# A decoder layer on one core: a quarter of the dense expert placed between the first two experts, the last additions on VectorE, the last outputs loaded into other buffers

## The chip, the core and the metric

The kernel runs on one core of a Trainium2 chip. A core has five engines with queues of their own: TensorE (PE; its weight loads are PEld), VectorE (DVE), ScalarE (ACT), GpSimd (POOL) and SyncE (SP), which here only starts DMAs. The metric is the device time of one execution in microseconds; the median of several executions is given.

## What is computed

One pre-norm decoder layer over 16 x 64 = 1024 tokens of width 256: self-attention with block-scaled weights, cross-attention over a context with rotary embedding, and a mixture-of-experts feed-forward part. Only the last part matters here:

```python
scores = softmax(xt @ Wg.T)                 # 16 experts
topi = top_k(masked by the best 2 of 4 groups, 4)
h = silu(einsum('td,eid->eti', xt, W1)) * einsum('td,eid->eti', xt, W3)
y = einsum('etd,te->td', einsum('eti,edi->etd', h, W2), combine)
z = silu(xt @ Ws1.T) * (xt @ Ws3.T) @ Ws2.T
return y + z                                # added to x
```

Each token is served by 4 of the 16 experts. `y` is the sum of their outputs with the routing weights.

## The kernel before

The tokens lie in eight tiles of 128 rows, `x[0]` to `x[7]`, two halves of four. All products are made of float32 numbers split into a high part (rounded) and a low part (the rest): a product of two is three matmuls, so each matrix that TensorE reads has to be cast by ScalarE (`parts_of`, `weight_parts`) and subtracted by VectorE or GpSimd.

Fifteen of the sixteen experts work on gathered rows. GpSimd scatters each token's normalized row to slots of the expert (`xd` in DRAM, `send`, line 842), 384 slots for each; expert `e` loads its slots (`expert_inputs`, line 1253), turns them on TensorE (line 1265), multiplies them with its up-weights (`expert_hidden`, line 1273), multiplies with its down-weights (`expert_output`), and scatters the result rows to `yd` in DRAM (`send_outputs`, line 1291). `yd` holds, for each token, its four choices. They are loaded back (`load_outputs`, line 1314) and added to `x` with their routing weights (`add_outputs`, line 1327).

The sixteenth expert, `w_last`, is the dense expert: it is computed for all tokens and added with a weight that is zero where it was not chosen (`add_last`, line 952). Its first half is done before the expert loop. The second half is two quarters of 256 tokens, `dense_hidden(w_last, 1, 0)` and `dense_hidden(w_last, 1, 1)`. Quarter 0 adds to `x[4]` and `x[5]`, quarter 1 to `x[6]` and `x[7]`.

The loop `for e in range(E + 1)` (line 1353) is a software pipeline: at step `e` it prepares the inputs and weights of expert `e`, does the up-products of expert `e-1`, and the outputs of expert `e-2`. The instructions are placed by a scheduler that models the engines; `tc.issue_after(ins)` keeps what stands in its block behind an instruction in that order. `up_done[0]` is the last up-product made so far, `gated[0]` the last instruction of `expert_hidden`, `lows[-1]` the last subtraction of a low part.

Three kinds of buffers matter:

- accumulators for up-products, `mm`, four banks, of which an expert takes three;
- accumulators for outputs, `av`, two banks (`av_tile`), which are used by `send_outputs` and by `dense_output`;
- `got`, nine buffers of 256 rows each, for the outputs that are loaded back (16 loads in all, so the last seven wait for a buffer); `w123`, two buffers of 128 x 1280 for raw expert weights, each free once the weights have been cast and subtracted.

Up to nine loads can run ahead. The loads of choice `k` depend on all scatters of `yd` so far (`behind(got, returned)`); the last choice's loads depend on the last expert's scatter. All of them are started from SP's queue.

Of the kernel before, what the change touches and what calls it, by code (L numbers as in the profile page):

```python
# [25 lines left out]
F32 = mybir.dt.float32  # L26
# [3 lines left out]
AF = mybir.ActivationFunctionType  # L30
ALU = mybir.AluOpType
AX = mybir.AxisListType

B, S, D = 16, 64, 256
NT = B * S
NI = NT // 128
# [6 lines left out]
E, INTER, NGRP, TOPK, TOPKG = 16, 176, 4, 4, 2  # L43
# [4 lines left out]
W_COLS = W_UP + 2 * D  # L48
# [23 lines left out]
def decoder_layer(ctx: ExitStack, tc: tile.TileContext, a: dict, out: bass.AP):  # L72
    nc = tc.nc
# [17 lines left out]
    def av_tile():  # L91
        return ps_av.tile([128, 512], F32, tag="av", name="av")
# [18 lines left out]
    def parts_of(src, hi, lo, eng=None):  # L111
        nc.scalar.copy(hi, src)  # L112
        return (eng or nc.vector).tensor_tensor(lo, src, hi, ALU.subtract).ins
# [3 lines left out]
    x = [t[:, i, :] for t in x_pairs for i in range(2)]  # L117
# [131 lines left out]
    def behind(read, writes):  # L249
        for w in writes:  # L250
            tc.add_manual_dep(
                read,
                w.name,
                mybir.DependencyInfo(mybir.DependencyClass.Sync, mybir.DependencyReason.DATA),
                reason="it reads rows of each",
            )
# [29 lines left out]
    def expert_up(w, xs, n):  # L286


        ps = [mm_tile(cols=n) for _ in range(3)]
        return ps, [expert_up_part(k, w, xs, t) for k, t in enumerate(ps)][-1]  # L290
# [8 lines left out]
    def expert_output(ps, w, h_p, cols):  # L299


        w2 = [[p[:, W_UP + k * D : W_UP + (k + 1) * D] for p in w] for k in range(2)]
        h = [p[:, cols] for p in h_p]
        return matmuls(
            ps,
            [
                (h[0], w2[0][0]),
                (h[0], w2[0][1]),
                (h[1], w2[0][0]),
                (h[2], w2[1][0]),  # L310
                (h[2], w2[1][1]),
            ],
        )

    with ExitStack() as attn:
# [643 lines left out]
        with (  # L959
# [109 lines left out]
            def dense_weights():  # L1069

                parts = [
                    xw.tile([128, 2, 2, 4 * HQ], F32R, tag=f"w_q{n}", name=f"w_last{n}")
                    .rearrange("p a b c -> p (a b c)")[:, :W_COLS]
                    for n in range(2)
                ]
                up = xb.tile([128, 3, 2, 2, DC], F32, tag="w_s", name="w_last_up")
                down = xb.tile([128, 2, D], F32, tag="w_o0", name="w_last_down")
                for t, cols in (
                    (up.rearrange("p a b c d -> p (a b c d)"), slice(0, W_UP)),
                    (down.rearrange("p a b -> p (a b)"), slice(W_UP, W_COLS)),  # L1080
                ):
                    nc.sync.dma_start(out=t, in_=a["W123"][E - 1][:, cols])
                    parts_of(t, parts[0][:, cols], parts[1][:, cols])
                return parts
# [18 lines left out]
            def dense_gated(g, up, g2, up2):  # L1103
                h_p = [
                    xa.tile([128, 512], F32R, tag=f"roped1{n}", name=f"dense1{n}", bufs=1)
                    for n in range(2)
                ]
                h_p.append(xa.tile([128, 512], F32R, tag="q_r", name="dense2"))
                nc.vector.tensor_tensor(g, up, g, ALU.mult)
                parts_of(g, h_p[0], h_p[1])  # L1110
                nc.vector.tensor_tensor(g2[:64], up2[64:], g2[64:], ALU.mult)
                parts_of(g2[:64], h_p[2][:64], h_p[2][64:])
                return h_p
# [15 lines left out]
            for n in range(len(units) + 2):  # L1129
# [58 lines left out]
                if n == 8:  # L1188
                    w_last = dense_weights()
                    with after(exps[-1]):  # L1190
                        routed.append(weights_of_choices(0))
                if n == 9:
# [30 lines left out]
                    with after(aimed, placed):  # L1223
# [4 lines left out]
                        h_p = dense_gated(*dense_ups)  # L1228
# [4 lines left out]
    fw = ctx.enter_context(tc.tile_pool(name="fw", bufs=2, reuse_waits="tile"))  # L1233
    fx = ctx.enter_context(tc.tile_pool(name="fx", bufs=2, reuse_waits="tile"))
    fh = ctx.enter_context(tc.tile_pool(name="fh", bufs=2, reuse_waits="tile"))
    fy = ctx.enter_context(tc.tile_pool(name="fy", bufs=2, reuse_waits="tile"))

    gated, up_done = [None], [None]
# [34 lines left out]
    def expert_hidden(w, xs, n):  # L1273


        ps, up_done[0] = expert_up(w, xs, n)
        g, h, g2, h2 = (
            fh.tile([128, SLOTS], F32, tag=tag, name=tag)[:, :n] for tag in ("g", "h", "g2", "h2")
        )
        h_p = [  # L1280
            fh.tile([128, SLOTS], F32R, tag=tag, name=tag)[:, :n] for tag in ("hp0", "hp1", "hp2")
        ]
        nc.scalar.activation(g, ps[0], AF.Silu)
        nc.vector.tensor_tensor(h, ps[1], g, ALU.mult)
        parts_of(h, h_p[0], h_p[1])
        silus.append(nc.scalar.activation(g2[64:], ps[2][:64], AF.Silu).ins)
        nc.vector.tensor_tensor(h2[:64], ps[2][64:], g2[64:], ALU.mult)
        gated[0] = parts_of(h2[:64], h_p[2][:64], h_p[2][64:])
        return h_p
# [23 lines left out]

    def load_outputs(k):

        tiles = []
        for n in range(NI // 2):
            t = fy.tile([128, 2, D], F32, tag="got", name="got", bufs=9)
            first = (E - 1) * SLOTS + (TOPK - 1 - k) * NT + n * 256
            got = nc.sync.dma_start(  # L1320
                out=t, in_=yd[first : first + 256].rearrange("(i p) d -> p i d", p=128)
            ).ins
            behind(got, returned)
            tiles.append(t)
        return tiles

    def add_outputs(k, got, cw):
        for i in range(NI):
            y, w = got[i // 2][:, i % 2], cw[i // 4][:, k, i % 4 : i % 4 + 1]
            if i % 3 == 2:  # L1330
                nc.scalar.activation(y, y, AF.Copy, scale=w)
                nc.gpsimd.tensor_tensor(x[i], x[i], y, ALU.add)
            else:
                nc.vector.scalar_tensor_tensor(x[i], y, w, x[i], ALU.mult, ALU.add)  # L1334

    def dense_hidden(w, half, n):
        return expert_hidden(w, [p[:, :, n * 256 : n * 256 + 256] for p in normed[half]], 256)

    def dense_output(w, h_p, half, n, add):
        for b in range(2):  # L1340
            ps = av_tile()[:, :D]
            expert_output(ps, w, h_p, slice(b * 128, b * 128 + 128))
            add(half, 2 * n + b, ps)
# [6 lines left out]
    ws, xs, hs, got = {}, {}, {}, {}  # L1350
    with tc.issue_after(lows[-1]), tc.issue_after(silus[-1]):
        ws[0] = expert_weights(a["W123"][0], nc.vector)
    for e in range(E + 1):
        if e in (1, 2):

            low = lows[-1]
            hs[e - 1] = expert_hidden(ws[e - 1], xs[e - 1][0], SLOTS)
        if e < E - 1:
            low = lows[-1]
            with tc.issue_after(up_done[0] if e in (1, 2) else low):  # L1360
                xs[e] = expert_inputs(e)
            if e >= 1:
                with tc.issue_after(low), tc.issue_after(silus[-1]):
                    ws[e] = expert_weights(a["W123"][e], nc.vector if e < 3 else nc.gpsimd)
        if e == 1:
            with tc.issue_after(gated[0]), tc.issue_after(silus[-1]):
                routed.append(weights_of_choices(1))
        if 0 <= e - 1 < E - 1 and e > 2:
            hs[e - 1] = expert_hidden(ws[e - 1], xs[e - 1][0], SLOTS)
        if e - 2 >= 0:  # L1370
            if e == E:

                with tc.issue_after(gated[0]):
                    h_p = dense_hidden(w_last, 1, 0)
            last = send_outputs(e - 2, ws.pop(e - 2), hs.pop(e - 2), xs.pop(e - 2)[1])
            if e - 2 == E - TOPK - 2:
                short = slots_are_short()
            k = e - 2 - (E - 1 - TOPK)
            if k >= 0:
                got[k] = load_outputs(k)  # L1380
    with ExitStack() as behind_last:
        for ins in (*last, gated[0]):
            behind_last.enter_context(tc.issue_after(ins))
        cw = [r[0] for r in routed]
        add_outputs(0, got[0], cw)
        dense_output(w_last, h_p, 1, 0, add_last)
        add_outputs(1, got[1], cw)
        dense_output(w_last, dense_hidden(w_last, 1, 1), 1, 1, add_last)
        for k in range(2, TOPK):
            add_outputs(k, got[k], cw)  # L1390
    for i in range(NI):
        (nc.sync if i % 2 == 0 else nc.scalar).dma_start(
# [10 lines left out]
    with tc.If(short > 0):  # L1403
        w_over = [weights_without_slot(half, routed[half][2]) for half in range(2)]
        with tc.For_i(0, E - 1, 1) as e:
            w = expert_weights(a["W123"][bass.ds(e, 1)].rearrange("o p c -> p (o c)"))
            for half in range(2):
                dense_expert(w, half, add_over)

                t = fs.tile([128, 4, E], F32, tag="slot", name="w_next")  # L1410
# [105 lines left out]
```

## Time and profile before

| What | Value |
|---|---|
| median of 3 runs | 580.62 us (577.94 to 586.16) |
| profiled execution, its own time | 577.4 us |
| span of the profiled execution | 575.5 us |
| mean granted TensorE clock | 0.978 |
| first expert's up-products begin | 454.54 us |
| second expert's up-products begin | 463.24 us |
| third expert's up-products begin | 471.41 us |
| first addition of a loaded output | 552.59 us |
| last scatter of expert outputs started | 556.00 us |
| VectorE's last addition ends | about 571.2 us |

Times inside the profile count from the start of the span. In the profile's lines L104 is the helper through which nearly all matmuls go, so that one has to look at the tiles: `mm<-xs,w` are an expert's up-products, `mm<-xn,w_last` those of the dense expert, `av<-w,hp` an expert's outputs, `av<-w_last,hp` the dense expert's. A number in brackets at the end of a line is the time for which the engine was idle before it, and what ended that.

### The profile page before, as it was taken

To read this page: it belongs to the slowest core of one execution; us is meant where nothing else is said; L and a number is where in the kernel's file an instruction comes from. 1 tells how busy PE (TensorE), PEld (TensorE's weight loads), DVE (VectorE), ACT (ScalarE), POOL (GpSimd) and SP (SyncE) were. 2 spreads that over 40 slices of the span, in tenths; PEclk is the share of its full clock that TensorE was granted. 3 is DMA by queue.
4 is the path that set the end of the run, shared out by engine and by line. 5 is a ranking of instruction groups with operands and counts; after the bars stand their busy time and mean duration, and the time that the engine had idled before them with its cause. 6 is when DMAs were issued, how large, how long until landed. Compare 5 with 4: busy or idle time off the path is not lost.

```text
span 575.5 us, 10603 instructions
## 1 busy us (share of the span) xinstructions
PE 540.3 (94%) x4013; PEld 446.7 (78%) x4013; DVE 400.2 (70%) x879; ACT 279.3 (49%) x524; POOL 230.6 (40%) x213
## 2 busy tenths in 40 slices
PE   7999999999999989999999999999999779999962
PEld 5889898888989876757778577685787669999951
DVE  6355566644655788848577586889777479999866
ACT  4677557575574431230432323152525187777551
POOL 4260500101001005426243444632544717888862
PEclk9999999999999999999999999999999789999995
DMA  8564431823200599482020000000511658777384
GB/s 227 145 166 146 111 109 39 227 86 112 75 1 1 167 250 308 111 239 52 2 70 1 8 1 1 0 31 0 188 50 68 202 169 285 240 245 238 122 279 152
DMA packets 56294, 70.83 MB, mean 123 GB/s; under 512 B 13872, under 2 KB 42768, under 8 KB 56240
## 3 DMA queue, kind: packets, MB, share of 16 engines
q1 hardware_dynamic: 51408, 58.71, 34.5%
q0 software_dynamic: 3696, 10.36, 4.7%
q10 hardware_dynamic: 1136, 1.05, 0.6%
q8 instruction: 33, 0.54, 0.4%
q14 instruction: 21, 0.17, 0.1%
HBM read 48.61 MB, written 21.86 MB: 122 GB/s over the span
## 4 chain that ended last, share of the span: by engine, by line
PE 81%; DVE 7%; issue 4%; DMA 3%; ACT 3%; POOL 1%; SPq 1%; DVEq 0%; ACTq 0%; POOLq 0%
PE mm L104 47%; PE mm L1005 7%; PE av L590 5%; PE av L104 5%; PE at L573 4%; PE at L343 3%; PE at L1028 2%; PE av L1041 2%; PE at L1265 2%; PE mm L439 2%; DMA bqkv<-in_bqkv 1%; PE mm L461 1%; DMA got<-yd 1%; DVE x L1334 1%; POOL roped L990 1%
## 5 line engine op out<-in xcount | busy, mean ns | idle before, releaser
L990 POOL TENSOR_TENSOR roped<-rt,rt 128x512 f32<-128x512 f32 x48 | 62.6, 1325 | 83.4 <-DVE rt L984 80.5
L984 DVE TENSOR_TENSOR rt<-mm,rope_q 128x512 f32<-128x512 f32 x96 | 61.4, 685 | 24.3 <-PE mm L104 23.6
L104 PE MATMUL mm<-xn,w_q 128*128 128x512 f32 x288 | 73.9, 403 | 0.5 <-ACT xn L222 0.5
L104 PEld LDWEIGHTS mm<-xn,w_q 128*128 128x128 f32 x288 | 52.2, 188 | 14.0 <-issue 1.8
L104 PE MATMUL mm<-xs,w 128*128 128x384 f32 x270 | 55.3, 354 | 7.0 <-ACT xs L112 5.8
L1304 POOL DMA_INDIRECT yd<-y,to x45 | 47.9, 1064 | 27.6 <-ACT y L1299 13.1
L104 PEld LDWEIGHTS mm<-xs,w 128*128 128x128 f32 x270 | 48.4, 198 | 9.0 <-ACT xs L112 6.6
L327 ACT ACTIVATE p<-p 128x512 f32<-128x512 f32 x32 | 20.1, 629 | 62.3 <-DVE p L326 62.3
L324 DVE TENSOR_REDUCE sm_m<-at 128x8 f32<-128x512 f32 x32 | 21.8, 680 | 37.1 <-PE at L573 36.2
L1005 PE MATMUL mm<-roped,w_s 128*64 128x512 f32 x192 | 46.4, 602 | 0.7 <-POOL roped L990 0.7
L522 POOL TENSOR_TENSOR wv<-code,scale 128x512 fp32r<-128x512 f32 x7 | 9.5, 1360 | 88.2 <-DMA scale<-in_scales 58.7
L613 DVE TENSOR_TENSOR x<-mm,x 128x256 f32<-128x256 f32 x64 | 26.0, 419 | 23.9 <-PE mm L104 21.9
L104 PE MATMUL mm<-wo,o 128*128 128x256 f32 x256 | 39.6, 295 | 0.0
L104 PE MATMUL av<-w,hp 128*128 128x256 f32 x225 | 35.2, 290 | 0.7 <-ACT y L1299 0.7
L104 PE MATMUL mm<-xn,wq 128*128 128x512 f32 x128 | 34.6, 405 | 0.7 <-ACT xn L222 0.5
L104 PE MATMUL mm<-wv,xn 128*128 128x256 f32 x256 | 35.2, 289 | 0.0
L104 PE MATMUL mm<-xn,wk 128*128 128x512 f32 x128 | 34.9, 404 | 0.0
L590 PE MATMUL av<-pt,v 128*128 128x128 f32 x256 | 34.5, 277 | 0.0
L104 PEld LDWEIGHTS mm<-wo,o 128*128 128x128 f32 x256 | 32.9, 190 | 1.5 <-issue 0.4
L590 PEld LDWEIGHTS av<-pt,v 128*128 128x128 f32 x256 | 32.0, 191 | 1.2
L104 PEld LDWEIGHTS mm<-wv,xn 128*128 128x128 f32 x256 | 31.8, 189 | 0.9
L104 PEld LDWEIGHTS av<-w,hp 128*128 128x128 f32 x225 | 30.6, 190 | 1.9 <-ACT y L1299 1.2
(216 smaller groups left out, 1145.8 us busy)
## 6 DMA issues: line engine op xcount, KB each, us to landing
w<-in_W SPq DMA_DIRECT2D x15, 640.0 KB
code<-in_codes SPq DMA_DIRECT2D x32, 256.0 KB
scale<-in_scales SPq DMA_DIRECT2D x32, 256.0 KB
xr<-xd SPq DMA_DIRECT2D x15, 408.0 KB
xd<-zeros SPq DMA_DIRECT2D x8, 720.0 KB
yd<-zeros SPq DMA_DIRECT2D x8, 512.0 KB
got<-yd SPq DMA_DIRECT2D x16, 256.0 KB
wq<-in_Wq SPq DMA_DIRECT2D x4, 512.0 KB
```

The source lines that it names most:

```text
L104: m = nc.tensor.matmul(ps, lhsT=l, rhs=r, start=(n == 0), stop=(n == len(pairs) - 1))
L324: nc.vector.tensor_reduce(m, sc, AX.X, ALU.max)
L327: exps.append(nc.scalar.activation(p, p, AF.Exp, scale=scale).ins)
L343: last = nc.tensor.transpose(ps[:, 2 * n : 2 * n + 2, :].rearrange("p a q -> p (a q)"), pn[:, 2 * n : 2 * n + 2, :].rearrange("p a k -> p ...
L439: nc.tensor.matmul(ps[:, c * DCQ : (c + 1) * DCQ], lhsT=wq[:, h, c * 128 : (c + 1) * 128], rhs=wkq[:, h, :], start=True, stop=True,)
L573: nc.tensor.matmul(sc[par * 64 : par * 64 + 64, 2 * g + pp, :], lhsT=qk[0][:, b * S : (b + 1) * S], rhs=qk[1][:, b * S : (b + 1) * S], sta ...
L590: nc.tensor.matmul(av[:, k * 128 : (k + 1) * 128], lhsT=v[:, i, k0 : k0 + HD], rhs=pt[:, i].rearrange("p a q -> p (a q)"), start=True, sto ...
L613: nc.vector.tensor_tensor(x[i], ps, x[i], ALU.add)
L984: nc.vector.tensor_tensor(mt, ps3, rope_table(t, 2 * ab + k), ALU.mult)
L990: nc.gpsimd.tensor_tensor(r.rearrange("p (b s) -> p b s", s=S), one, two, op)
L1005: nc.tensor.matmul(ps[h // 2][(h % 2) * 64 : (h % 2) * 64 + 64], lhsT=w_s[:, t, blk, ab, :], rhs=roped[2 * t + ab], start=first[h], stop=l ...
L1304: sent = nc.gpsimd.indirect_dma_start(out=yd[: (E - 1) * SLOTS + min(TOPK, E - 1 - e) * NT], out_offset=bass.IndirectOffsetOnAxis(ap=to[:, ...
```

## The change

One quarter of the dense expert (tokens of `x[4]` and `x[5]`) moves: its up-products now stand behind the first expert's, its outputs ahead of the first expert's outputs. The other quarter takes the place that the first one had beside the last expert. All additions of loaded outputs are done by VectorE; before, every third one was a scaling on ScalarE and an addition on GpSimd. The last choice's outputs are loaded into the two raw weights' buffers, four loads of which two start from ScalarE's queue. The order of the additions at the end is changed accordingly. The number of loads, additions and products stays the same.

```diff
     def load_outputs(k):
 
-        tiles = []
-        for n in range(NI // 2):
-            t = fy.tile([128, 2, D], F32, tag="got", name="got", bufs=9)
+        if k == TOPK - 1:
+            tiles = [
+                t[:, n * 2 * D : (n + 1) * 2 * D].rearrange("p (i d) -> p i d", i=2)
+                for t in (fw.tile([128, W_COLS], F32, tag="w123", name="got_last") for _ in range(2))
+                for n in range(2)
+            ]
+        else:
+            tiles = [
+                fy.tile([128, 2, D], F32, tag="got", name="got", bufs=9) for _ in range(NI // 2)
+            ]
+        for n, t in enumerate(tiles):
             first = (E - 1) * SLOTS + (TOPK - 1 - k) * NT + n * 256
-            got = nc.sync.dma_start(
+            got = (nc.scalar if k == TOPK - 1 and n % 2 else nc.sync).dma_start(
                 out=t, in_=yd[first : first + 256].rearrange("(i p) d -> p i d", p=128)
             ).ins
             behind(got, returned)
-            tiles.append(t)
         return tiles
 
     def add_outputs(k, got, cw):
         for i in range(NI):
             y, w = got[i // 2][:, i % 2], cw[i // 4][:, k, i % 4 : i % 4 + 1]
-            if i % 3 == 2:
-                nc.scalar.activation(y, y, AF.Copy, scale=w)
-                nc.gpsimd.tensor_tensor(x[i], x[i], y, ALU.add)
-            else:
-                nc.vector.scalar_tensor_tensor(x[i], y, w, x[i], ALU.mult, ALU.add)
+            nc.vector.scalar_tensor_tensor(x[i], y, w, x[i], ALU.mult, ALU.add)
...
             hs[e - 1] = expert_hidden(ws[e - 1], xs[e - 1][0], SLOTS)
+            if e == 1:
+                with tc.issue_after(up_done[0]):
+                    h_p = dense_hidden(w_last, 1, 0)
...
             if e == E:
 
                 with tc.issue_after(gated[0]):
-                    h_p = dense_hidden(w_last, 1, 0)
+                    h_p = dense_hidden(w_last, 1, 1)
+            if e == 2:
+                dense_output(w_last, h_p, 1, 0, add_last)
             last = send_outputs(e - 2, ws.pop(e - 2), hs.pop(e - 2), xs.pop(e - 2)[1])
...
         cw = [r[0] for r in routed]
-        add_outputs(0, got[0], cw)
-        dense_output(w_last, h_p, 1, 0, add_last)
-        add_outputs(1, got[1], cw)
-        dense_output(w_last, dense_hidden(w_last, 1, 1), 1, 1, add_last)
-        for k in range(2, TOPK):
+        dense_output(w_last, h_p, 1, 1, add_last)
+        for k in range(TOPK):
             add_outputs(k, got[k], cw)
```

## The prediction

> **What bounds the kernel now.** I read the page's busy rows first, then busy time by stage, then the engines' timelines at the two places that the change touches, then the waits.
>
> ```profile
> PE 540.3 (94%) x4013; PEld 446.7 (78%) x4013; DVE 400.2 (70%) x879; ACT 279.3 (49%) x524; POOL 230.6 (40%) x213
> ```
>
> TensorE is the bound over the span as a whole, but two stages differ from that mean. Busy time by stage (stage, its length, then busy time and count of PE, PEld, DVE, ACT, POOL; granted clock; DMA share; GB/s):
>
> ```profile
> 459.20:463.20 4.00, 0.81 (x7) 0.57 (x5) 1.95 (x3) 2.28 (x5) 1.69 (x2) 1.00 0.62 210
> 463.20:469.20 6.00, 5.88 (x26) 5.65 (x27) 4.35 (x17) 4.49 (x7) 0.00 (x0) 0.72 0.71 249
> ...
> 484.00:540.00 56.00, 55.22 (x377) 54.07 (x377) 52.91 (x90) 41.49 (x88) 46.76 (x38) 1.00 0.68 229
> ...
> 560.00:566.00 6.00, 1.99 (x6) 1.43 (x6) 5.87 (x10) 2.08 (x5) 3.10 (x4) 0.50 0.75 232
> 566.00:571.20 5.20, 1.22 (x4) 0.93 (x4) 5.12 (x12) 0.51 (x1) 0.95 (x1) 0.50 0.48 159
> ```
>
> From 484 to 540 us TensorE has no slack: what arrives late there stays late. Between the first two experts it stands idle for 3.2 us. After 560 us VectorE (5.87 of 6.00, 5.12 of 5.20) sets the end. The idle stretch in TensorE's timeline, and ScalarE's work in it:
>
> ```profile
> 459.19 0.82 PE L1265 MATMUL at<-ident,xr 128*128 128x128 f32 x6
> 463.24 0.79 PE L104 MATMUL mm<-xs,w 128*128 128x384 f32 x3 [3.23 <-ACT xs L112]
> ...
> 471.41 0.80 PE L104 MATMUL mm<-xs,w 128*128 128x384 f32 x3 [1.10 <-ACT xs L112]
> ```
> ```profile
> 460.57 0.48 ACT L1286 ACTIVATE g<-mm 64x384 f32<-64x384 f32 x1 [1.33 <-PE at L1265]
> 461.08 1.26 ACT L278 CAST w<-w 128x1280 fp32r<-128x1280 f32 x1
> 462.70 0.48 ACT L112 CAST xs<-at 128x384 fp32r<-128x384 f32 x1 [0.37 <-remote]
> ```
>
> The second expert's up-products wait for its cast rows, which stand in ScalarE's queue behind the first expert's second silu and a weight cast. In the tail, VectorE beside GpSimd, and the loads of the last choice:
>
> ```profile
> 552.59 3.65 DVE L1334 SCALAR_TENSOR_TENSOR x<-got,cw,x 128x256 f32<-128x256 f32 x9
> ...
> 563.39 1.83 DVE L1334 SCALAR_TENSOR_TENSOR x<-got,cw,x 128x256 f32<-128x256 f32 x2
> ```
> ```profile
> 563.22 1.71 POOL L1332 TENSOR_TENSOR x<-x,got 128x256 f32<-128x256 f32 x2 [0.88 <-DVE x L952]
> ```
> ```profile
> 561.03 1.90 SPq L1320 DMA_DIRECT2D got<-yd  x4
> ```
> ```profile
> 564.62 0.51 ACT L1331 ACTIVATE got<-got,cw 128x256 f32<-128x256 f32 x1 [2.43 <-DMA got<-yd]
> 566.12 0.51 ACT L1331 ACTIVATE got<-got,cw 128x256 f32<-128x256 f32 x1 [1.00 <-DMA got<-yd]
> ```
>
> An addition alone takes 0.41 us (3.65 for nine), beside a GpSimd addition 0.92 (1.83 for two). The last choice's loads start at 561.03, once the last expert's scattered rows have landed; the second of them lands at 564.6, the third at 566.1, and the fourth, by the same step, near 566.8. VectorE ends at 571.2, the stores at 575.5.
>
> **Part 1, the quarter moved forward.** It issues 18 up-products and 10 output products of 256 columns, two silus, two casts and six VectorE instructions. At the end 18 such products took 2.32 us, about 0.12 each, so 28 are 3.3 us of TensorE. In the built order the 18 follow the first expert's up-products and precede the second's transposes: 459.3 to 461.4, then transposes until 462.1. The idle time is not filled to its end, because ScalarE's queue grows too: after the silu that ends at 461.05 come the expert's first cast (0.5), the quarter's first silu (0.36), the expert's second cast (0.5) and the quarter's second silu (0.38). The last of these waits for TensorE; the silu at 460.57 came 1.2 us after its products, so I let this one start at 462.6. Then weight cast (1.26), the quarter's cast (0.41), rows cast (0.48): 465.1 instead of 463.18. The second expert's products begin 1.9 us late. Its low half waits for VectorE, where the weights' subtractions (1.56) now end near 465.8.
>
> A second wait is new. The quarter's two outputs take both of the output accumulators, and release them through two VectorE additions (0.4 each) that stand behind the second expert's silus and the last routing weights. The first expert's 15 output products, of which 10 ran in gaps between 463.9 and 472.4, all come after that, near 472. That is 1.2 us of TensorE (10 at 0.12) pushed past the same gaps.
>
> Bounds for the delay with which TensorE reaches the full loop: 0 if all 3.3 us fit in the 3.23 and 1.10 of idle time; +3.3 if none does. I take +2.0, near the 1.9 of the ScalarE sum. From the third expert's products on, the order on every engine is as before, so the delay is carried through to 552. SP's queue keeps its order; the fourth expert's weight load (464.36) waits for a raw buffer that comes free 1.9 us later, and is not used until the cast at 473.25, nine us after it: nothing. If that cover were gone, it would cost those 1.9 us again.
>
> The clock: TensorE was granted 0.72 in 463.20:469.20, right behind the 3.23 us of idleness, which costs 6.0 x 0.28 = 1.7 us. [...] By the row, a gap remains (462.1 to about 464.7), a further one stands near 471, and even a 3.23 us gap brought the drop: sum +2.0. I use the row and keep -1.7 for the range.
>
> **Part 2, additions by VectorE alone.** Removed: 8 of 32 additions on GpSimd with their ScalarE scalings, 2 of 4 dense additions of the tail, four gating instructions (0.42 each) on VectorE. Added: 8 additions on VectorE. Its tail is now 34 x 0.405 = 13.8 us. Before, it was busy 5.43 + 5.87 + 5.12 = 16.4 of the 18.6 us from 552.6 to 571.2. From 552.6 work alone would end at 566.4, a gain of 4.8. ScalarE and GpSimd lose work on which only the scaled additions and the stores of their rows waited.
>
> Waits decide instead. Six additions run until 555.0; the second dense output needs an accumulator freed by the copy at 555.35, so VectorE passes its addition near 557.5. The second choice's last loads landed at 557.85 and 558.6 before; the third choice's four are in by about 562, as two of them no longer wait for buffers that GpSimd had to release (issued about 1.5 us earlier). So all but the last choice is added by about 563.3, the last pair of the third choice apart.
>
> **Part 3, the last loads.** The raw weights' buffers are free since GpSimd's last subtraction (542.81 + 1.34), so these loads wait only for the scattered rows, at 561.0 as before. ScalarE has nothing behind them but stores. [...] four issues in 1.90 us are halved, at most 0.95 gained[...]. The row has 232 GB/s in this stage, 1 MB, so the last landing is bandwidth more than issue. Without any gain the fourth lands at 566.8, and four additions end the work at 568.4 (-2.8); with the full 0.95 at 567.5 (-3.7). The third choice being out of the way earlier also frees bandwidth, so I take -3.7; bounds -1 (landings 1.7 us later, as four loads meet) and -4.8 (VectorE's work alone). The last stores take 4.3 us either way.
>
> **Sum.** 575.5 + 2.0 - 3.7 = 573.8 us of span, -0.3%. The profiled execution took 577.4 us including 1.9 around its span, 3.2 below the median of 580.62. In proportion: 580.62 x 573.8 / 575.5 = 579.
>
> **Rivals.** (a) *The gap swallows the quarter and the clock stays up*: delay 0, clock -1.7, tail -4.8: -6.5, median 574. For it: 4.3 us of idle time against 3.3 of work. Against: ScalarE's queue is what TensorE waits for, and it gets longer. (b) *Slower: the first output accumulators become the wait.* TensorE stands behind two VectorE additions near 470 to 472, which stand behind two table loads (1.28 each) and two silus. No work is absorbed (+3.3) and a further 6.8 us at half speed costs 3.4; the tail, held by landings, gives -2.7: +4.0, median 585. It decides once the loop is entered more than 3.7 us late. Against it: the same 1.1 us gap at 470.3 brought no drop of clock. (c) *The tail does not do what it says*: all four last loads share the same bandwidth, land late, and VectorE waits: -1 and +2.0, median 581.6.
>
> **Numbers.** Forecast 0.60 (own range 575.5 to 582.5), (a) 0.13, (b) 0.17, (c) 0.10. The three times shown lie 1.4% apart, which adds about 2 us either way, so the range is 573.5 to 585.5. About 2% (11.6 us) is what a measurement of this kernel tells from no change. No case reaches it; I leave 0.05 on either side for what the trace doesn't show, such as the clock at half speed in the full loop.
>
> **What would show it.** Right: TensorE idle near 462 to 464.7 with the quarter's products ahead of it; the second expert's products at about 465; the loop about 2 us late at 484; no VectorE addition of 0.8 us or more in the tail; the last addition 3 to 4 us closer to the last expert's scatter. Wrong: the second expert's products before 464 or after 467; VectorE idle for over 3 us after the scatter has landed; the last loads landing over 6 us after their issue.

## The result, and the profile after

| | before | after |
|---|---|---|
| median of 20 executions each | 577.22 us | 581.04 us |
| span of the profiled execution | 575.5 us | 579.2 us |
| first expert's rows turned on TensorE (begin) | 451.61 us | 453.27 us |
| second expert's up-products begin | 463.24 us | 467.11 us |
| fifth expert's up-products, the group of 13, begin | 484.06 us | 489.44 us |
| last scatter's issue ends | 557.07 us | 562.37 us |
| last choice's loads begin to be issued | 561.03 us | 567.71 us |
| VectorE's last addition ends | about 571.2 us | 574.74 us |

The ratio is 1.0073 (95% interval 1.0059 to 1.0087): the change costs 4.2 us, where the forecast had a gain of 1.7. The medians in this table are of all executions, and the ratio leaves out those that ran in a slower state, some 10 us longer (5 of 20 before, 3 of 20 after). TensorE is the bound over the span as before, in the first row of busy times of the page:

```profile
PE 539.9 (93%) x4013; PEld 447.6 (77%) x4013; DVE 400.2 (69%) x887; ACT 275.6 (48%) x516; POOL 224.6 (39%) x205
```

The same stages as in the prediction, the last one drawn out to VectorE's new end (stage, its length, busy time and count of PE, PEld, DVE, ACT, POOL; granted clock; DMA share; GB/s):

```profile
459.20:463.20 4.00, 4.00 (x19) 4.00 (x18) 0.97 (x2) 1.40 (x4) 1.92 (x2) 0.61 0.53 168
463.20:469.20 6.00, 4.15 (x28) 3.39 (x27) 5.07 (x11) 5.05 (x10) 0.00 (x0) 1.00 0.41 130
484.00:540.00 56.00, 55.19 (x383) 54.34 (x382) 52.17 (x88) 41.54 (x87) 45.27 (x38) 1.00 0.73 242
560.00:566.00 6.00, 0.69 (x5) 0.48 (x5) 5.97 (x16) 0.00 (x0) 2.06 (x2) 0.89 1.01 336
566.00:574.80 8.80, 0.00 (x0) 0.00 (x0) 6.82 (x17) 0.00 (x0) 0.00 (x0) 0.50 0.67 215
```

The first row looks as if the idle time had been filled. It hasn't: TensorE ran those 4 us at a clock of 0.61, with products most of which had been done by then in the kernel before. Its timeline shows where its time went:

```profile
456.11 6.13 PE L104 MATMUL mm<-xs,w 128*128 128x384 f32 x18 [1.36 <-DVE x L948]
462.03 2.44 PE L104 MATMUL mm<-xn,w_last 128*128 128x256 f32 x18
...
466.53 0.74 PE L104 MATMUL av<-w_last,hp 128*128 128x256 f32 x4 [1.40 <-ACT hp L112]
467.11 0.69 PE L104 MATMUL mm<-xs,w 128*128 128x384 f32 x3
...
474.87 0.86 PE L104 MATMUL av<-w,hp 128*128 128x256 f32 x5 [2.13 <-DVE x L952]
```

The first expert's 18 up-products take 6.13 us at half clock (4.82 before, at half clock for the most part). The quarter's 18 follow, then a wait of 1.40 for ScalarE, and later one of 2.13 for VectorE's additions of the quarter (L952), because its outputs hold both output accumulators. ScalarE's queue in that place:

```profile
464.51 0.38 ACT L1286 ACTIVATE g<-mm 64x256 f32<-64x256 f32 x1 [0.54 <-PE mm L104]
464.91 1.26 ACT L278 CAST w<-w 128x1280 fp32r<-128x1280 f32 x1
466.08 0.40 ACT L112 CAST hp<-h 128x256 fp32r<-128x256 f32 x1
466.38 0.85 ACT L112 CAST xs<-at 128x384 fp32r<-128x384 f32 x2
```

Silu of the quarter, weight cast, cast of the quarter, cast of the second expert's rows: the order that was forecast, 1.9 us behind the forecast's times. In the tail, VectorE's timeline and SP's queue:

```profile
559.07 2.86 DVE L1337 SCALAR_TENSOR_TENSOR x<-got,cw,x 128x256 f32<-128x256 f32 x7
...
563.54 5.22 DVE L1337 SCALAR_TENSOR_TENSOR x<-got,cw,x 128x256 f32<-128x256 f32 x13
570.69 2.46 DVE L1337 SCALAR_TENSOR_TENSOR x<-got_last,cw,x 128x256 f32<-128x256 f32 x6 [1.92 <-DMA got_last<-yd]
573.07 0.88 DVE L1337 SCALAR_TENSOR_TENSOR x<-got,cw,x 128x256 f32<-128x256 f32 x2
573.86 0.88 DVE L1337 SCALAR_TENSOR_TENSOR x<-got_last,cw,x 128x256 f32<-128x256 f32 x2
```
```profile
567.71 0.87 SPq L1328 DMA_DIRECT2D got_last<-yd  x2
```

Every addition now takes 0.41 us, as forecast; VectorE then waits 1.92 us for the last loads. From the issue of those loads to the last addition it is 7.0 us (567.71 to 574.74) instead of 10.1. But they start 5.3 us after the last scatter's issue ended, instead of 4.0.

So the profiled pair adds up: the last scatter is 5.3 us late, 1.7 of it come back behind it, and the span is 3.7 longer. Two things don't fit. The first expert's rows are turned 1.66 us later, and on TensorE no changed instruction stands ahead of them. And the waits between 440 and 464 us hold long ones that end on "issue", which means that the engine waited for nothing that the profile shows (engine, line, releaser: us in total, times, longest):

```profile
ACT g L1283 <- issue: 4.6, 1, 4.6
DVE h L1284 <- issue: 4.5, 1, 4.5
...
PE mm L104 <- issue: 3.0, 1, 3.0
```

The trace holds no record of an engine's semaphore change for 5.4 us from 445.7 and for 5.1 us from 457.2 (before: gaps of 4.0, 2.2, 4.8 and 1.8 us in that stretch). Such a gap is not all standstill: VectorE's product at 461.70 uses the silu that ScalarE ended at 461.54, inside the second gap, and no record of that signal exists. So records are missing, and how long the engines' signals really stood still is not shown. That engines started late is shown by their own rows.

TensorE's clock is a further part of the loss. The same stage in the two profiles, before and after:

```profile
476.00:484.00 8.00, 8.00 (x60) 7.97 (x59) 7.20 (x15) 6.46 (x14) 5.13 (x6) 1.00 0.92 292
476.00:484.00 8.00, 8.00 (x49) 7.97 (x48) 6.67 (x15) 4.82 (x12) 5.66 (x5) 0.79 0.68 198
```

In the same busy time TensorE did 49 products instead of 60. Ahead of the full loop its clock was halved from 450.8 to 457.6 and from 464.5 to 467.9 us before, and from 452.1 to 462.3 and from 475.9 to 479.4 after. From 440 us, where the two are at the same place within 0.2 us, to the fifth expert's group of 13, TensorE was busy for 36.27 us before and 41.06 after, of which 8.71 and 12.09 at half clock; it was idle for 7.79 and 8.38. So the 5.4 us by which the loop is entered later are 3.1 of work (in the main the quarter's products), 1.7 of clock (half of the added time at half clock) and 0.6 of idle time.

The experiments had to tell apart the change's own cost from the rest.

### The profile page after: what moved, and what is told of

Read it like the earlier page. It is cut to its first block, busy times and chain, and to the rows that moved or that the text cites. A ratio compares the mean times of both kernels' runs of the same rounds, so it can differ in the third digit from the quotient of the medians.

```text
span 579.2 us, 10587 instructions
## 1 busy us (share of the span) xinstructions
PE 539.9 (93%) x4013; PEld 447.6 (77%) x4013; DVE 400.2 (69%) x887; ACT 275.6 (48%) x516; POOL 224.6 (39%) x205
## 4 chain that ended last, share of the span: by engine, by line
PE 82%; DVE 6%; DMA 3%; issue 3%; ACT 2%; POOL 1%; another core or an unknown queue 0%; POOLq 0%; SPq 0%; DVEq 0%; ACTq 0%
PE mm L104 49%; PE mm L1005 6%; PE av L104 5%; PE av L590 5%; PE at L573 4%; PE at L343 3%; PE at L1028 2%; PE av L1041 2%; PE mm L439 2%; PE at L1265 2%; DMA bqkv<-in_bqkv 1%; DMA yd<-y,to 1%; PE mm L461 1%; POOL roped L990 1%; ACT w L278 1%
```

## The experiments

Medians and ratios, both of the same executions, with the kernel before in the same comparison:

| kernel | median, us | before, us | ratio (95% interval) |
|---|---|---|---|
| q_only | 580.86 | 572.87 | 1.0147 (1.0127 to 1.0166) |
| adds_only | 572.16 | 572.87 | 0.9998 (0.9982 to 1.0013) |
| loads_only | 573.32 | 572.87 | 1.0010 (1.0001 to 1.0020) |
| adds_loads | 573.24 | 572.87 | 1.0007 (0.9993 to 1.0021) |
| after_2 | 570.46 | 570.01 | 1.0005 (0.9993 to 1.0017) |
| no_quarter | 568.34 | 570.01 | 0.9972 (0.9962 to 0.9982) |
| q_behind | 571.19 | 570.01 | 1.0021 (1.0008 to 1.0033) |
| after_3 | 570.85 | 569.76 | 1.0014 (1.0005 to 1.0024) |
| q_only_2 | 572.45 | 569.76 | 1.0043 (1.0029 to 1.0057) |
| own_later | 573.26 | 569.76 | 1.0057 (1.0038 to 1.0076) |
| q_ahead | 570.46 | 569.76 | 1.0007 (0.9994 to 1.0020) |
| before_late | 579.18 | 569.62 | 1.0162 (1.0139 to 1.0186) |
| after_late | 578.14 | 569.62 | 1.0153 (1.0130 to 1.0175) |
| q_ahead_late | 578.84 | 569.62 | 1.0165 (1.0136 to 1.0193) |
| after_4 | 570.44 | 569.65 | 1.0010 (1.0001 to 1.0019) |
| no_quarter_2 | 568.48 | 569.65 | 0.9971 (0.9960 to 0.9983) |
| own_bufs | 569.50 | 569.65 | 0.9999 (0.9991 to 1.0006) |

before_2 is one execution of the kernel before (569.23 us), for its profile.

### One part at a time

q_only moves the quarter and keeps the tail's additions and loads as they were; adds_only, loads_only and adds_loads keep the quarter at the end.

```diff
 # q_only: in the loop and at the end
+            if e == 1:
+                with tc.issue_after(up_done[0]):
+                    h_p = dense_hidden(w_last, 1, 0)
...
-        dense_output(w_last, h_p, 1, 0, add_last)
+        dense_output(w_last, h_p, 1, 1, add_last)
         add_outputs(1, got[1], cw)
-        dense_output(w_last, dense_hidden(w_last, 1, 1), 1, 1, add_last)
 # adds_only: in add_outputs
-            if i % 3 == 2:
-                nc.scalar.activation(y, y, AF.Copy, scale=w)
-                nc.gpsimd.tensor_tensor(x[i], x[i], y, ALU.add)
-            else:
-                nc.vector.scalar_tensor_tensor(x[i], y, w, x[i], ALU.mult, ALU.add)
+            nc.vector.scalar_tensor_tensor(x[i], y, w, x[i], ALU.mult, ALU.add)
 # loads_only: load_outputs as in the change; adds_loads: both
```

> Only the quarter is moved; additions and last loads stay as before. Theory A (the quarter enters the loop about 4 us late, and the tail gives part of it back): TensorE enters the full loop 3 to 5 us late, the tail is shorter by 1.5 to 2.5 us (four gating instructions and two additions less on VectorE), so 1 to 3 us slower than before. Theory B (my forecast: 2 us late, the quarter's absence from the tail worth about as much): within 1 us of before. Theory C (the loss of the whole change sits in the tail): as fast as before or faster.

> Only the additions by VectorE alone; the quarter, the buffers and the queue of the last loads stay as before. Theory A: VectorE's additions fall from 0.9 to 0.4 us where GpSimd worked beside them, and it has 8 more of them: 0 to 2 us faster. Theory C (earlier release of the buffers lets the third choice's loads collide with the last scatter): the last scatter lands 1 us or more later, so no gain, or up to 2 us slower.

> Only the last choice's four loads into the raw weights' buffers, two of them from ScalarE's queue; additions and quarter stay. All theories: the last scatter sets when these loads may start, so within 1 us of before; if the second queue helped bandwidth too, 1 to 2 us faster.

> The additions and the last loads together, without the quarter: the whole change but its first part. Theory A: 1 to 4 us faster than before, since the loss of the whole change lies at the quarter. Theory C: slower than before by 2 us or more, the last scatter landing over 5 us after its issue, as in the changed kernel (5.2 us there, 3.9 us before).

In this comparison the loss is the quarter's. It is 8.4 us, more than any of the theories had (1 to 3 at most). The additions, alone or with the loads, change nothing that can be told from zero, so theory A's 1 to 4 us of gain for adds_loads failed too; the loads alone cost 0.1%, at the edge of their interval. TensorE and ScalarE in q_only:

```profile
463.50 1.22 PE L104 MATMUL av<-w_last,hp 128*128 128x256 f32 x4 [5.96 <-ACT hp L112]
...
465.91 4.34 PE L104 MATMUL mm<-xs,w 128*128 128x384 f32 x15
```
```profile
461.49 0.38 ACT L1286 ACTIVATE g<-mm 64x256 f32<-64x256 f32 x1 [4.91 <-remote]
```

The quarter's second silu starts 4.6 us after its products (they end at 456.88), TensorE stands for 5.96 us, and its clock is halved for 6.8, from 462.5. That made a theory: ScalarE's queue ahead of the second expert's casts, and the clock behind the hole. It had to explain 8 us where the whole change costs 4.

### The whole change again, and without the quarter

```diff
 # no_quarter, against the change: the quarter isn't computed
-            if e == 1:
-                with tc.issue_after(up_done[0]):
-                    h_p = dense_hidden(w_last, 1, 0)
...
-            if e == 2:
-                dense_output(w_last, h_p, 1, 0, add_last)
 # q_behind, against the change: the quarter's up-products behind the second expert's casts
         if e == 1:
+            with tc.issue_after(lows[-1]):
+                h_p = dense_hidden(w_last, 1, 0)
```

> The kernel before, once more, for a second profile of the stretch between the first two experts. Theory A (the 3.2 us of TensorE idle time there, which the forecast filled with the quarter, belonged to one disturbed execution): the idle time between the first expert's up-products and the second's is about 1 us, no stretch at half clock between 450 and 470 us, span 569 to 572. Theory B (the idle time is always there): 3 us idle and a half-clock stretch again, span 573 to 576.

> The whole change, beside the kernel before on the chip on which its parts are compared. Theory A (the quarter in the head costs about 8 us wherever the head ran undisturbed before; the new tail is worth 0 to 1 us without it): 1.012 to 1.016. Theory C (the new tail gives back half of what the quarter costs, since VectorE's additions wait for nothing once the quarter has left): 1.005 to 1.009.

> The changed kernel with the quarter left out altogether (rows 512 to 767 get nothing of the dense expert): what the tail gains when the quarter leaves it, with nothing put into the head. Its distance to the changed kernel is the price of the quarter in the head. Theory A: the tail gains 0 to 2 us, ratio to before 0.996 to 1.000, and the quarter costs 7 to 9 us. Theory C: the tail gains 4 us, ratio 0.992 to 0.994, the quarter costs 8 us all the same. The forecast's own sum had 3.7 us (0.9936) and 2.0 us.

> The changed kernel with the quarter issued behind the second expert's input and weight casts instead of ahead of them; the same products. Theory A1 (the price comes from ScalarE's queue: the second expert's casts stand behind the quarter's silus, TensorE runs dry for 6 us and its clock drops): the second expert's up-products start at most 3 us later than in the kernel before, no long idle stretch, ratio 1.002 to 1.006. Theory A2 (the price is the work itself and the accumulators: TensorE has no idle time to give in the head): the same as the changed kernel within 1.5 us.

The whole change now costs nothing that can be told from zero, so theory A's 8 us fall, and theory C was too much as well. TensorE in before_2:

```profile
453.90 0.85 PE L1265 MATMUL at<-ident,xr 128*128 128x128 f32 x6 [1.32 <-DMA xr<-xd]
454.98 0.80 PE L104 MATMUL mm<-xs,w 128*128 128x384 f32 x3 [0.24 <-ACT xs L112]
...
461.34 0.85 PE L1265 MATMUL at<-ident,xr 128*128 128x128 f32 x6 [1.61 <-DMA xr<-xd]
462.98 0.79 PE L104 MATMUL mm<-xs,w 128*128 128x384 f32 x3 [0.33 <-ACT xs L112]
```

and in after_2:

```profile
452.51 2.31 PE L104 MATMUL mm<-xn,w_last 128*128 128x256 f32 x18
...
456.87 0.73 PE L104 MATMUL av<-w_last,hp 128*128 128x256 f32 x4 [1.40 <-ACT hp L112]
457.43 0.69 PE L104 MATMUL mm<-xs,w 128*128 128x384 f32 x3
...
465.21 0.86 PE L104 MATMUL av<-w,hp 128*128 128x256 f32 x5 [2.13 <-DVE x L952]
```

The second expert's up-products start 8.3 us earlier in before_2 than in the first profile (454.98 for 463.24). There is no half clock ahead of the loop, and the only sizeable idle stretches are waits for gathered rows (1.32 and 1.61). In after_2 the two waits that the quarter brings, 1.40 and 2.13, are the same as in the first profile of after. The fifth expert's group of 13 starts at 476.00 in before_2 and 478.41 in after_2: the head costs 2.4. From 440 us to there TensorE was busy for 30.49 and 33.45 us, never at half clock, and idle for 5.51 and 4.96. So of the 5.4 us of the first pair 3.0 are not in this one, and 1.7 of them are clock and 1.1 idle time. These are single executions (569.23 and 568.50 us, the changed kernel the faster one), so the ratios decide: the quarter in the head costs 0.33% or 1.9 us (1.0005 against 0.9972), and the tail without it gains 0.28% or 1.6 us. With q_behind, the casts come first and the second expert starts at 455.37, nearly as early as before, yet it is no faster than the whole change: the queue on ScalarE isn't the price.

Why the new tail is worth 1.6 us here and nothing in adds_loads shows in VectorE's end. In adds_loads:

```profile
559.89 1.68 DVE L1337 SCALAR_TENSOR_TENSOR x<-got_last,cw,x 128x256 f32<-128x256 f32 x4 [0.33 <-DMA got_last<-yd]
...
562.27 0.87 DVE L952 SCALAR_TENSOR_TENSOR x<-av,cl,x 128x256 f32<-128x256 f32 x2
...
564.64 0.88 DVE L1337 SCALAR_TENSOR_TENSOR x<-got_last,cw,x 128x256 f32<-128x256 f32 x2
```

and in after_2:

```profile
558.05 2.46 DVE L1337 SCALAR_TENSOR_TENSOR x<-got_last,cw,x 128x256 f32<-128x256 f32 x6 [0.17 <-DMA got_last<-yd]
560.43 0.87 DVE L1337 SCALAR_TENSOR_TENSOR x<-got,cw,x 128x256 f32<-128x256 f32 x2
561.23 0.87 DVE L1337 SCALAR_TENSOR_TENSOR x<-got_last,cw,x 128x256 f32<-128x256 f32 x2
```

From the first last-choice addition on, VectorE never waits; 14 additions take 5.6 us with the quarter still at the end, 10 take 4.1 without it. Taking work off GpSimd and ScalarE is paid for by VectorE until the quarter leaves. adds_loads was measured in the first comparison of parts and no_quarter in the second, but a later pair agrees: with the quarter moved in both, the new additions and loads make 1.6 us (q_only_2 against after_3, 572.45 and 570.85).

### The same kernels once more, and three other places for the quarter

```diff
 # own_later, against the change: intermediates in tiles of their own (four free `got` buffers),
 # output products behind the first expert's
-                    h_p = dense_hidden(w_last, 1, 0)
+                    h_q = hidden_apart(w_last, 1, 0)
...
-            if e == 2:
-                dense_output(w_last, h_p, 1, 0, add_last)
             last = send_outputs(e - 2, ws.pop(e - 2), hs.pop(e - 2), xs.pop(e - 2)[1])
+            if e == 2:
+                with tc.issue_after(last[-1]):
+                    dense_output(w_last, h_q, 1, 0, add_last)
 # q_ahead, against the change
-            hs[e - 1] = expert_hidden(ws[e - 1], xs[e - 1][0], SLOTS)
             if e == 1:
-                with tc.issue_after(up_done[0]):
+                with tc.issue_after(silus[-1]):
                     h_p = dense_hidden(w_last, 1, 0)
+            hs[e - 1] = expert_hidden(ws[e - 1], xs[e - 1][0], SLOTS)
```

> The whole change a third time, so that the kernels of this call stand beside it under the same conditions. Theory D (the price of the quarter in the head depends on the execution: about 2 us where the engines' signals in the head come at once, 4 us and more where they stop for 1 to 5 us at a time and TensorE's clock halves; the new tail gives 1.7 us back): 1.000 to 1.002 where the kernel before takes about 570 us, 1.005 to 1.009 where it takes 573 us or more. Theory E (the change itself brings the stops): always 1.005 or more.

> The quarter alone in the head, with the tail of the kernel before, once more. Theory D: its head is the same as the whole change's, so beside a kernel before of about 570 us it takes 0 to 2 us more than the whole change (1.001 to 1.005), and the 1.0147 of its first measurement came with the stopped signals and the halved clock. Theory E' (moving the quarter without the new tail costs 8 us wherever it runs): 1.013 to 1.016 again.

> The whole change with the quarter's intermediates in tiles of their own and its output products issued behind the first expert's outputs, so that neither accumulator nor hidden tile of the first expert waits for VectorE's additions of the quarter. Theory F (part of the quarter's 1.9 us in the head is the wait of 2.13 us of TensorE for the quarter's additions, which take both accumulators): that wait is gone, and 1 to 2 us are saved against the whole change. Theory G (the wait lies beside other waits, for the second expert's casts): within 0.6 us of the whole change.

> The whole change, but with the quarter's up-products ahead of the first expert's instead of behind them, where TensorE waits 1.9 us for the first expert's rows when the kernel before is undisturbed, and 3.5 to 5 us when it isn't. Theory H (the idle time ahead of the first expert is real in every execution, and filling it also keeps TensorE's clock up): 1 to 3 us faster than the whole change, ratio to before 0.994 to 0.999. Rival (ScalarE and VectorE, which have the first expert's casts and the routing there, become late): as the whole change or slower.

q_only_2 is the kernel of q_only, and it costs 2.4 us instead of 8.4 (0.43% and 1.47%). Its TensorE at the same place:

```profile
456.91 0.74 PE L104 MATMUL av<-w_last,hp 128*128 128x256 f32 x4 [1.40 <-ACT hp L112]
...
459.12 2.88 PE L104 MATMUL mm<-xs,w 128*128 128x384 f32 x15
```

The hole of 5.96 us is one of 1.40, and the 15 products take 2.88 us instead of 4.34. ScalarE's silu, 4.6 us late in q_only, here starts as its products end (454.89). q_only reached the group of 13 at 486.69, q_only_2 at 478.44: of these 8.3 us the longer hole is 4.6, and 6.8 us at half clock are up to 3.4. One program has both prices, so most of what q_only showed first wasn't the price of the quarter in itself. The two ran on different chips, numbered 7 and 5, but before_2 and after_2, without such late starts, ran on number 7 too.

own_later misses theory F and theory G: it is 2.4 us slower than after_3. The wait for VectorE is gone, and a longer one took its place (TensorE, then ScalarE):

```profile
469.58 1.32 PE L104 MATMUL mm<-xs,w 128*128 128x384 f32 x3 [4.60 <-ACT xs L112]
```
```profile
467.89 1.26 ACT L278 CAST w<-w 128x1280 fp32r<-128x1280 f32 x1 [1.62 <-DMA w<-in_W]
```

The rows' cast stands behind a weight cast that waits for its load; TensorE idles 4.60 us and the clock is halved for 6.8 us. q_ahead gains nothing that can be told from zero over after_3: the quarter's products start only at 448.27, and push the first expert from 447.3 to 450.5. Its loop is entered at the same time as after_3's (the group of 13 at 478.45 in both).

### A hole made on purpose

```diff
 # before_late, and the same in after_late and q_ahead_late: two small loads ahead of the first expert's rows
+        idle = []
+        if e == 0:
+            pad = fx.tile([128, 16], F32, tag="pad", name="pad", bufs=1)
+            for _ in range(2):
+                idle.append(nc.sync.dma_start(out=pad, in_=xd[first : first + 128, :16]).ins)
...
+        behind(load, idle)
```

> The kernel before, with two small loads (128x16 of the same rows) chained ahead of the load of the first expert's rows, so that TensorE stands idle for about 6 us before the first expert instead of 2, as in the first profile of before (3.5 us). Theory J (a hole of that length is what halves TensorE's clock there): a stretch of 6.8 us at half clock near 450 to 458, and 5 to 8 us lost (4 of delay, 1 to 4 of clock): 1.009 to 1.014. Rival K (the half clock of the first profile had another cause): 4 us lost, no half clock: 1.005 to 1.008.

> The whole change with the same two loads ahead of the first expert's rows. Theory J (with the clock halved as the loop is entered, the quarter's 28 products cost twice and the change loses 3 to 5 us against the kernel before with the same hole): 1.015 to 1.023, 3 to 5 us over the other. Rival K (the hole delays both alike, and the change costs what it costs without it, 0.3 to 1 us): within 1.5 us of the kernel before with the hole.

> The whole change with the quarter's up-products ahead of the first expert's, and the same two loads ahead of the first expert's rows. Theory J (the products fill part of the hole, and the clock stays up or drops for less): 2 to 5 us faster than the whole change with the same hole. Rival K: as the whole change with the hole, within 1.5 us.

The hole was longer than meant. TensorE in before_late and in after_late:

```profile
455.09 1.54 PE L1273 MATMUL at<-ident,xr 128*128 128x128 f32 x6 [8.23 <-DMA xr<-xd]
```
```profile
455.42 1.54 PE L1273 MATMUL at<-ident,xr 128*128 128x128 f32 x6 [8.51 <-DMA xr<-xd]
```

The price of the hole itself, 1.0162, is above what both theories had. Both clocks were halved for 10.2 us, from inside the hole on (about 451 us in before_late, 449 in after_late), and before_late's for another 3.4 from 475.0; both reach the group of 13 at the same time (487.00 and 487.06). The changed kernel is not slower than the kernel before with the same hole: 578.14 against 579.18. So theory J falls: a late first expert alone doesn't make the change cost more. It doesn't clear the half clock, though. The two kernels were not halved for the same time: 13.7 us before and 10.2 after, where the first pair had 10.2 before and 13.7 after. Putting the quarter into the hole (q_ahead_late) didn't help either.

### Once more, and the shared tiles

own_bufs takes `hidden_apart` alone from own_later; the order of the products is that of the change.

> The whole change a fourth time. Theory D (the change costs 0.3 to 0.8 us where the signals in the head come at once, and about 4 us where they stop for 1 to 5 us at a time): 1.000 to 1.002 if the kernel before takes about 570 us here, 1.005 to 1.009 if it takes 573 us or more and its first expert starts later than 449 us. Rival K (what was seen once at 1.0073 won't come back, whatever the kernel before takes): 0.999 to 1.002 in both cases.

> The whole change with the quarter left out (rows 512 to 767 get nothing of the dense expert), beside the whole change of the same call. Theory D: 0.996 to 0.998, so that the quarter in the head costs about 2 us; where the signals stop and the kernel before takes 573 us or more, the same 0.996 to 0.998 and the quarter costs 5 us or more. Rival K: 2 us in both cases.

> The whole change with the quarter's intermediates in tiles of their own, so that the second expert's hidden tiles don't wait until the first expert's output products have read theirs; the order of the products is kept. Theory F (that wait is part of the 1.9 us): 0.5 to 1.5 us faster than the whole change. Theory G (the accumulators and the work are all of it): within 0.5 us of it.

The kernel before took 569.65 us, so what disturbed the first comparisons did not come back, and the part of the expectations that speaks of them stays untested. The rest holds: the quarter costs 0.39% or 2.2 us in the head, the tail gains 0.29%. own_bufs gets 0.6 us of it back by the ratios (0.9 by the medians), at the edge of what the intervals tell apart. The wait for VectorE's additions, in own_bufs and in after_4:

```profile
466.02 0.86 PE L104 MATMUL av<-w,hp 128*128 128x256 f32 x5 [1.64 <-DVE x L952]
```
```profile
466.57 0.86 PE L104 MATMUL av<-w,hp 128*128 128x256 f32 x5 [2.12 <-DVE x L952]
```

No version beat the kernel before; own_bufs is level with it.

## Why the prediction was wrong, step by step

The step that failed in every comparison is the tail: forecast at -3.7, it gave -1.6 or -1.7. With the head at +2.0, which the undisturbed comparisons bear out, this alone turns the forecast gain of 1.7 us into a loss of about 0.4. The rest of the recorded 4.2 us came in the main in the head of that comparison: 1.7 us of added half clock, which the forecast had put at nothing, and 1.1 of idle time that did not fill as in the later pair.

**The tail, -3.7.** Mis-sized. The working had 6.5 us from the issue of the last loads to the last addition (561.0 to 567.5, against 10.1 before), because only four additions were to stand behind the fourth landing. In fact ten additions, 4.05 us of VectorE's work, stand behind the first landing: eight of the last choice and the third choice's last pair. In the first pair that landing came 3.0 us after the issue, which makes 7.0; in the second 3.9, which makes 8.0 against 10.7 (554.12 to 562.10, 552.11 to 562.81). In after_2 the last loads have landed by 559.5, but VectorE can't end sooner. In the first pair the loads also began 1.4 us later behind the scatter, which the working had put at "as before"; 1.7 were left. By the ratios, the gain is 1.6. The second queue for these loads gained nothing by itself (loads_only, 1.0010). A slip that didn't matter: "by the same step" the fourth landing would be 567.6, not 566.8.

**The head, +2.0.** In the comparison that it was made for, the loop was entered 5.4 us late (484.06 to 489.44), 1.7 of it present before the first changed product, 3.7 behind. In the profiles without late starts the term was right: 2.4 there, 1.9 and 2.2 by the ratios. What it rested on was partly wrong all the same. The 3.23 us of idle time that the quarter was to fill came from one such disturbed execution; in before_2 the idle time lies in two waits for rows. And the ScalarE sum of 1.9 us agreed with the result by luck: q_behind and q_ahead avoid that queue and are no cheaper. Of the 3.3 us of products about a third is absorbed, wherever in the head they stand.

**The second wait** was named rightly: 2.13 us of TensorE for VectorE's L952. Removing it (own_later) moved the idle time to the next cast.

**The clock.** The prediction kept the half clock behind the hole of 3.23 us as it was and added nothing. That stretch went away (1.00 in 463.20:469.20), but the one ahead of it, 6.8 us long before, became 10.2, and another 3.4 us came at 476: 1.7 us lost. Such stretches belong to the execution more than to the kernel: after_2 and after_3 have none ahead of the loop and after_4 has 3.4 us (the second expert's 15 products took 4.27 us there, 2.87 in after_2), no_quarter none and no_quarter_2 3.4. Nor did the drop need a hole as long as the one of 3.23: the one at 476 stands behind a hole of 2.13.

**The sum.** +2.0 and -1.6 give +0.4, and the later comparisons show +0.3 to +0.8 (1.0005, 1.0014, 1.0010). The rival that came nearest to the first comparison is (b): loop entered over 3.7 us late, the accumulators' wait, further half clock, tail -2.7 or less. The half clock is there, at half the size that (b) gave it (1.7 for 3.4). The wait of 2.13 us didn't make the difference, since it is in after_2 too, at no such cost.

**What stays open** is why the first comparison cost some 3.5 us more than the later ones. Shown is where: 3.0 us more in the head of the profiled pair, 1.7 of clock and 1.1 of idle time. It is no matter of single executions: all 20 of the changed kernel had mean clocks of 0.970 to 0.978, while after_2's had 0.982 to 0.987. q_only shows the same, 8.4 us once and 2.4 us once with one program, the larger with the late starts. Not shown: what makes the engines start late, and whether the change draws more of it or only met more.

## What to carry to other kernels

Slack read off one profiled execution may belong to that execution (the wait of 3.23 us for the second expert's cast rows in before was 0.24 in before_2): before filling a gap, look whether a second profile of the same kernel has it. Work moved into a phase with waits for arriving data (1.32 and 1.61 us in before_2) was absorbed here only to about a third of its 3.3 us, wherever in the phase it was put. Taking work off GpSimd and ScalarE onto VectorE, which ends last, gained only where VectorE lost other work at the same time: nothing that can be told from zero with the quarter still at the end (adds_loads, 1.0007), 1.6 us without it (after_3 against q_only_2).

## What the runs showed of the hardware

In the six profiles of the first comparison and of the parts (before, after, q_only, adds_only, loads_only, adds_loads) records of semaphore changes are fewer from 400 us on, where GpSimd's indirect DMAs run (the first at 405.07 us in before): 203 to 220 between 400 and 440 us, against 478 and 479 in before_2, after_2 and q_only_2; up to 400 us the counts agree (3521 in before and in after). In these comparisons the kernel before took 577.2 and 572.9 us, later 569.6 to 570.0, and the silu that starts 4.6 us late in q_only, and at once in q_only_2, stands in one of these profiles. What makes records go missing or engines start late, and whether the two belong together, no run here shows.

Ahead of the full loop TensorE's clock was halved for 6.8 and 3.4 us in before, and for 10.2 and 3.4 us in after. With idle stretches of 4.6 (own_later), 5.96 (q_only) and 8.2 us (before_late) it was halved for 6.8, 6.8 and 10.2 us, from before the end of the idle stretch. With shorter ones it varied: holes of 1.40 and 2.13 us brought no half clock in after_2 (1.00 from 447 to 469 us), while 3.4 us of it began behind holes of 1.40 in after_4 (1.9 us behind) and 2.13 in after (1.1), and at the end of one of 2.10 in no_quarter_2. The length of the hole alone doesn't tell whether the clock drops.
